# A two-layer mixer and expert network: mixers admitted at 0.9 of the pace, sums of squares closed one piece later, first expert weights and rows loaded earlier

## The chip, the cores and the metric

The kernel runs on one core of a Trainium2 chip. A core has five engines, each with its own queue of instructions that it works off in order: PE (matrix multiply; PEld is its weight load), DVE (VectorE), ACT (ScalarE), POOL (GpSimd) and SP (only transfers here). Transfers (DMA) are issued by SP, ACT and POOL. SBUF is the on-chip memory, PSUM the banks that PE writes, DRAM the chip's large memory. The metric is device time in microseconds (us).

## The reference

`x` has 4 sequences of 1024 tokens with 1024 channels, `f` (fside) the same shape. Two layers follow each other:

```
mix(L) = sigmoid(x or x1) * (nf + nb - ekv + euk*v) / (df + db - ek + euk) * (0.8 + 0.2 tf)
x1  = x + ((mix0 @ weight.T) * scale + bias)
h   = rmsnorm(mix1) * norm_w              # needs the sum of squares over all channels of a token
out = x1 + mix1 + sum over 4 of 32 experts + shared(h)
```

with k = v = f. `nf, df` are forward scans over the tokens (a = a*decay + ek), `nb, db` backward ones. The router takes the four best of 32 experts per token by `h @ router_w.T`; an expert is `(silu(h w1a) * (h w1b)) w2` with inner size 512, the shared one the same with 1024. All is float32.

## The kernel before, in words

**Tokens and channels.** Channels lie on the partitions, 8 tiles (NC) of 128. Tokens go in 8 chunks `q` of 512 (CH), two for each sequence `b`. PE works in *pieces*, most of them 16 matmul instructions of 128x128 by 128x512 into one PSUM bank: `first_ffn(q)` (8 pieces, L431, weights `w0t`, the mixer's output `c0` as moving side), `shared_up(q)` (16, L644) and `shared_down(q)` (8, L672).

**Mixers.** `mixing()` (from L234) is a generator over 64 units (sequence, channel tile, layer). A unit is two forward scans (L280), two backward scans (L292) and some passes on DVE, exponentials and logarithms on ACT, one accumulating transfer `fg<-euk` on POOL (L325), and a store to `c0_d` or `c1_d` in DRAM (L340). A unit of layer 0 also loads `xg` (L334, issued on ACT's queue) and takes its sigmoid on ACT (L223) at the start of the next step. Each `yield` gives the DVE time that the step is held to take (W_SCANS and so on).

**The written order.** Nothing is scheduled at run time. `run()` (L377) walks through the list of pieces from `order()` and writes instructions to the queues in that order. It keeps two running totals, `work["vector"]` and `work["tensor"]`: before each piece it lets mixer steps in while the first is below the second, then writes the piece, then what is due `after` so many pieces, then one step of each stream in `beside`. A piece's loads (`early`) are written two pieces ahead. `mix_until` writes mixer steps at once where a piece needs a unit that is not yet written.

**Gate and sum of squares.** `gate(q, ot, ...)` follows each piece of `first_ffn` (for chunks 0 and 1 it runs later, in `late_gate`): a sigmoid on ACT, a product on DVE into `c1` and its square on ACT (L465, L466), then two accumulating transfers on POOL: `c1` into the residual in DRAM (L469) and, but for chunk 0, the square into the tile `acc` (L473). All eight squares of a chunk go into the same `acc`. `total` then multiplies by ones on PE (L480), which gives the sum over partitions, and starts `norm_route(q)` in `beside`. For chunk 0, `total` is called for each of the eight tiles.

**norm_route(q)**, one step per piece: square root on ACT into `rs`, reciprocal on DVE (L523), the eight tiles scaled on DVE (L526, in two steps of four), the router matmul on PE (L533) and its copy on ACT (L535), then top four (L559, L560), ranks (`chose`, L596, L597), and in four steps `turn_rows`: PE transposes (L544) into the PSUM tiles `tr` (two buffers, also used by L533 and by `turned` of `shared_down`, L677), ACT copies (L546), stores to the row table `h_d`. At the end tokens and shares are scattered to expert slots.

**plan() and the experts.** After the last chunk's routing `plan()` works out which expert and which tokens each block of 128 rows has, in two kinds: pairs of blocks (kind 0) and single ones (kind 1). Then `first_weights` allocates the weight tiles and loads the weights of the first two units, 6 MB each, in six steps. After the pieces come an `If` (L1211) for surplus blocks, which are none in this data, and `run_units`: per unit a gather of the token rows `hs<-h_d` on POOL (L936), transposes (L951), 7 half-size products for gate and up (L1097), the same for down, and an indirect accumulate to DRAM.

**What the change touches by name:** pool sizes `pc0` (buffers of `c0`; 12) and `p1` (holds `rs`), `PACE`, `mix_until`, `run`, `gate`/`total`, `norm_route`, `plan`, `first_weights`, `order`, `Unit.gather`, `run_units`.

Of the kernel before, what the change touches and what calls it, by code (L numbers as in the profile page):

```python
# [8 lines left out]
FP = mybir.dt.float32  # L9
# [13 lines left out]
P = 128  # L23
CH = 512
# [7 lines left out]
def kernel(  # L32
# [157 lines left out]
    def right(name, bufs):  # L190
        return a.enter_context(tc.tile_pool(name=name, bufs=bufs, side="right"))
# [3 lines left out]
    p1 = right("p1", 1)  # L195
    p2 = right("p2", 2)
    pxg = right("pxg", 2)
    pc0 = right("pc0", 2 * NC - 4)
    pc1 = right("pc1", NC)
    px = right("px", 6)  # L200
    pw0 = right("pw0", 3)
# [8 lines left out]
    W_SCANS, W_MIN, W_PASS, W_HALF = 4.7, 0.7, 1.25, 0.75  # L210
    W_PIECE, W_SMALL = 6.9, 1.0
    LATENCY = 12.0
    table = [None]

    def exp_ln(to, of, func, **kw):
# [127 lines left out]


    work = {"vector": 0.0, "tensor": 0.0}
    mixer = mixing()

    def mix():
        step = next(mixer, None)
        if step is None:  # L350
            return False
        work["vector"] += step
        return True

    def mix_until(*wanted):
        while not made.issuperset(wanted):
            assert mix()
            work["tensor"] = max(work["tensor"], work["vector"])

    due = []  # L360
    count, told = [0], [0]
# [1 line left out]
    def after(pieces, f, vector=0.0, tensor=0.0):  # L363

        told[0] += 1
        due.append((count[0] + 1 + pieces, told[0], f, vector, tensor))
# [10 lines left out]
    def run(pieces, ahead=2):  # L377
        for i, piece in enumerate(pieces):
            for p in pieces[i : i + ahead + 1]:
                if p.early:  # L380
                    p.early()
                    p.early = None
            while work["vector"] < work["tensor"] and mix():
                pass
            piece.do()
            work["tensor"] += piece.tensor
            count[0] += 1
            now = sorted(d for d in due if d[0] <= count[0])
# [59 lines left out]
    def gate(q, ot, x, lag=1):  # L448

        b = q // NCH  # L450
        c1 = c1s[q, ot]
        held = {}

        def sigmoid():
            held["y"] = psq.tile([P, CH], FP, name="y")
            other(held["y"], x, AF.Sigmoid, bias=v["b0"][:, ot : ot + 1])


        each = q == 0
        if ot == 0 and not each:  # L460
            accs[q] = pacc.tile([P, CH], FP, name="acc")
        square = accs[q] if ot == 0 and not each else None

        def gated():
            nc.vector.scalar_tensor_tensor(c1, c1, nosc[:, b : b + 1], held["y"], ALU.mult, ALU.mult)  # L465
            nc.scalar.activation(held["y"] if square is None else square, c1, AF.Square)  # L466

        def add():
            nc.gpsimd.dma_start(out=resT_d[ot, :, bass.ts(q, CH)], in_=c1, accum_op=ALU.add)  # L469
            if each:  # L470
                total(held["y"])
            elif square is None:
                nc.gpsimd.dma_start(out=accs[q], in_=held["y"], accum_op=ALU.add)  # L473

        def total(of):
            if of is None:
                of = accs.pop(q)
            if ot == 0 or not each:
                sums[q] = ps_ss.tile([P, CH], FP, name="ss")
            nc.tensor.matmul(  # L480
                sums[q], lhsT=ones, rhs=of, start=(ot == 0 or not each), stop=(ot == NC - 1)
            )
            if ot == NC - 1:
                beside.append(norm_route(q))

        after(lag, sigmoid)
        after(lag + 1, gated, W_HALF)
        after(lag + (3 if each else 2), add, 0.0, W_SMALL if each else 0.0)
        if ot == NC - 1 and not each:
            after(lag + 3, lambda: total(None), 0.0, W_SMALL)  # L490

    def late_gate(q):

# [22 lines left out]
    def norm_route(q):  # L516

        NJ = CH // P
        hs = [c1s[q, ct] for ct in range(NC)]
        rs = p1.tile([P, CH], FP, name="rs")  # L520
        other(rs, sums.pop(q), AF.Sqrt, bias=eps_c, scale=1.0 / C)
        yield 0.0, 0.0
        nc.vector.reciprocal(rs, rs)  # L523
# [1 line left out]
        for ct in range(NC):  # L525
            nc.vector.scalar_tensor_tensor(hs[ct], hs[ct], v["nw"][:, ct : ct + 1], rs, ALU.mult, ALU.mult)  # L526
            if q == NT // CH - 1:
                nc.sync.dma_start(out=hT_d[ct], in_=hs[ct])
            if ct % 4 == 3:
                yield 4 * W_HALF, 0.0  # L530
        lgT_ps = ps_tr.tile([E, CH], FP, name="tr")
        for ct in range(NC):
            nc.tensor.matmul(lgT_ps, lhsT=rw_sb[:, ct, :], rhs=hs[ct], start=(ct == 0), stop=(ct == NC - 1))  # L533
# [163 lines left out]
    def plan():  # L697
# [5 lines left out]
        experts = lists.tile([1, 2, P], I32, name="experts")  # L703
        many = lists.tile([1, 3], I32, name="many")
        have.update(tokens=tokens, shares=shares, experts=experts, many=many)
        with tc.tile_pool(name="plan", bufs=1, side="right") as pl, tc.tile_pool(
            name="ps_pl", bufs=1, space=PSUM
        ) as ps_pl:
# [22 lines left out]
            for kind, n in enumerate((npair, nsing)):  # L731
# [47 lines left out]
                be_ps = ps_pl.tile([P, P], FP, name="pl_ps")  # L779
                nc.tensor.matmul(be_ps[0:1, :], lhsT=be, rhs=ident, start=True, stop=True)  # L780
                nc.vector.tensor_copy(experts[:, kind, :], be_ps[0:1, :])
                yield 0.3, 0.3
                for i, got in enumerate(gots):
                    tk_ps = ps_pl.tile([P, 2, P], FP, name="tk_ps")
# [3 lines left out]
                        )  # L788
                        nc.vector.tensor_copy(to[:, 2 * kind + i, :], tk_ps[:, o, :])
                    yield 0.6, 0.5  # L790
        beside.append(first_weights())


    NK, ND = NC // 2, NI // 2
# [64 lines left out]
        op(t[4], b21, t[2])  # L859
        yield  # L860

    def first_weights():
        pwt = kept.enter_context(tc.tile_pool(name="pwt", bufs=1, side="right"))
        have["w1"] = [
            [pwt.tile([P, NK, 2 * I], FP, name=f"w1_{at}{k}") for k in range(2)] for at in range(2)
        ]
        have["w2"] = [pwt.tile([P, NI, C], FP, name=f"w2_{at}") for at in range(2)]
        have["t_up"] = {i: pwt.tile([P, NK, I], FP, name=f"t_up{i}") for i in (2, 3, 4)}
        have["t_down"] = {i: pwt.tile([P, ND, 512], FP, name=f"t_down{i}") for i in (2, 3, 4)}
        for at in range(2):  # L870
            for _ in load(whole[at], at):
                yield 0.0, 0.0

    def order():

        pieces = first_ffn(0, False) + first_ffn(1, False) + late_gate(0)

        pieces.insert(-1, Piece(lambda: None, tensor=LATENCY / 3))
        pieces += [Piece(lambda: None, tensor=0.5) for _ in range(7)]
        up, gates = shared_up(0), late_gate(1)  # L880
        for i, piece in enumerate(up):
            pieces.append(piece)
            if i % 2 == 1:
                pieces.append(gates.pop(0))
        pieces += gates
        pieces += shared_down(0) + shared_up(1) + shared_down(1)
        pieces += first_ffn(2, True) + first_ffn(3, True) + shared_up(2) + shared_down(2) + shared_up(3)
        for b in range(2, B):
            q = NCH * b
            pieces += first_ffn(q, True) + first_ffn(q + 1, True) + shared_down(q - 1)  # L890
            pieces += shared_up(q) + shared_down(q)
            if b + 1 < B:
                pieces += shared_up(q + 1)
        return pieces
# [15 lines left out]
    with ExitStack() as m:  # L910
# [12 lines left out]
        class Unit:  # L923
# [6 lines left out]
                self.down_sums = sums_down(at) if self.kind == 0 else iter(())  # L930

            def gather(self):
                self.hs = []
                for i in self.lists:
                    hs = phs.tile([P, C], FP, name="hs")
                    nc.gpsimd.indirect_dma_start(  # L936
                        out=hs,
                        out_offset=None,
                        in_=h_d,
                        in_offset=bass.IndirectOffsetOnAxis(ap=tokens[:, i, self.n : self.n + 1], axis=0),  # L940
                    )
                    self.hs.append(hs)

            def turn(self):

# [191 lines left out]
        def rest_of(s):  # L1137
            for _ in s:
                pass

        def run_units(us, loaded, ahead=()):


            if not loaded:
                for u in us[:2]:
                    rest_of(u.load)
                rest_of(us[0].up_sums)
            us[0].gather()
            rest_of(us[0].turn())
            us[0].begin_left()  # L1150
            rest_of(us[0].left)
# [59 lines left out]
        with tc.If(count(2, MAXU[0] + MAXU[1]) > 0):  # L1211
            for kind in range(2):
                extra(kind, WHOLE[kind], count(kind, MAXU[kind]))
            with tc.manual_schedule(engines=ENG):
                for at in range(2):
                    rest_of(load(whole[at], at))
                rest_of(sums_up(0))

# [34 lines left out]
        with tc.manual_schedule(engines=ENG):  # L1253
            for u in main[:2]:
                u.load = iter(())
            main[0].up_sums = iter(())
            run_units(main, True, (ahead_1, ahead_2))

            o = have["w2"][before_last]
# [111 lines left out]
```

## Time and profile before

Median 5170.3 us of 3 runs (5169.01 to 5174.28). The profiled execution took 5172.99 us; its span, from first to last instruction, is 5171.2 us, so 1.8 us lie around it.

| stretch, us | what runs | PE busy of it | DVE busy | mean granted PE clock |
|---|---|---|---|---|
| 0 to 197 | mixers of sequence 0, no matmul | 0.0 | 183.9 | 1.00 |
| 197 to 357 | first layer of chunks 0 and 1, gates of chunk 0 | 130.0 of 160 | 140.6 | 0.88 |
| 357 to 1440 | pieces, with mixers beside them | 1015.4 of 1083 | 930.3 | 0.97 |
| 1440 to 2067 | pieces, mixers done | 620.8 of 627 | 104.9 | 1.00 |
| 2067 to 2085 | change to the experts | 0.3 of 18 | 8.6 | 0.59 |
| 2085 to 5121 | experts | 3029.1 of 3036 | 1750.8 | 1.00 |
| 5121 to 5171 | last chunk's shared part | 44.7 of 50 | 10.1 | 0.98 |

A line of a timeline reads: start, duration, engine, source line, operation, what it writes and reads, how many; in square brackets how long the engine had been idle before it and what ended that. In lists of waits, the three numbers are the sum in us, how often, and the longest.

### The profile page before, as it was taken

The page shows a single profiled execution, that of the slowest core. Times are in us where ns is not written, and L with a number is a line of the kernel's source. Part 1 is how long each engine was busy: PE and PEld are TensorE (multiplying, and loading weights), DVE is VectorE, ACT ScalarE, POOL GpSimd, SP SyncE. Part 2 cuts the span into 40 slices and gives each one's busy share as a digit, 9 for nine tenths or more (in the row PEclk, how much of TensorE's full clock was granted, in tenths as well). Part 3 has the DMA queues.
Part 4 walks back from the last instruction along what each step waited for, and adds up shares of the span by engine and source line. Part 5 has one row for each costly group of instructions (what it writes and reads, how often), then busy time and mean ns, then how long its engine had stood idle before and what let it go on. Part 6 is the DMA issues. An engine that isn't in the chain of part 4 may idle for free.

```text
span 5171.2 us, 36505 instructions
## 1 busy us (share of the span) xinstructions
PE 4840.2 (94%) x12906; PEld 2240.0 (43%) x12906; DVE 3129.2 (61%) x3280; ACT 1432.3 (28%) x1831; POOL 811.7 (16%) x765
## 2 busy tenths in 40 slices
PE   0478999999999999899999999999999999999999
PEld 0123443444444444444444444444444444444444
DVE  9978997899710221566655656565656556565621
ACT  5557666667510120111111111111111111111110
POOL 0113201411310120111111111111111111111100
PEclk9989999999999999999999999999999999999999
DMA  4678678679733854677777676767677777767684
GB/s 137 190 200 199 184 223 256 170 192 285 206 113 106 244 151 154 211 219 236 217 235 230 217 241 210 246 202 247 210 237 216 234 235 215 241 216 238 214 234 123
DMA packets 524210, 1077.76 MB, mean 208 GB/s; under 512 B 30641, under 2 KB 260146, under 8 KB 523410
## 3 DMA queue, kind: packets, MB, share of 16 engines
q1 hardware_dynamic: 386338, 744.70, 42.4%
q0 software_dynamic: 74656, 223.12, 20.6%
q10 hardware_dynamic: 63024, 107.50, 5.9%
q8 instruction: 105, 1.72, 0.1%
q14 instruction: 87, 0.71, 0.0%
HBM read 844.13 MB, written 203.56 MB: 203 GB/s over the span
## 4 chain that ended last, share of the span: by engine, by line
PE 86%; DVE 4%; DMA 4%; ACT 3%; issue 3%; ACTq 0%; POOL 0%; SPq 0%; POOLq 0%; DVEq 0%
PE gA L1097 14%; PE mm L644 13%; PE gB L1097 9%; PE gC L1097 9%; PE dA L1097 7%; PE mm L431 6%; PE mm L672 5%; PE dB L1097 5%; PE dC L1097 5%; PE tr L951 2%; PE gA L985 2%; PE gB L985 2%; PE tr L1034 1%; PE tr L533 1%; DMA xg<-in_xT 1%
## 5 line engine op out<-in xcount | busy, mean ns | idle before, releaser
L644 PE MATMUL mm<-c,wpc 128*128 128x512 f32 x1792 | 785.1, 597 | 8.4 <-issue 5.0
L431 PE MATMUL mm<-c,w0t 128*128 128x512 f32 x1024 | 454.9, 606 | 212.8 <-DMA w0t<-in_w 207.7
L644 PEld LDWEIGHTS mm<-c,wpc 128*128 128x128 f32 x1792 | 340.1, 192 | 429.7 <-issue 421.2
L1097 PE MATMUL gA<-w,hsT 128*128 128x512 f32 x1088 | 490.1, 593 | 0.0
L1097 PE MATMUL gB<-t_up,s_up 128*128 128x512 f32 x1088 | 489.1, 592 | 0.0
L1097 PE MATMUL gC<-w,s_up 128*128 128x512 f32 x1088 | 489.1, 592 | 0.0
L1081 POOL DMA_INDIRECT sum_d<-y,tokens x148 | 302.8, 2046 | 920.6 <-DMA sum_d<-y,tokens 542.8
L672 PE MATMUL mm<-sact,wpc 128*128 128x512 f32 x896 | 394.5, 595 | 9.6 <-DVE sact L653 9.6
L936 POOL DMA_INDIRECT hs<-h_d,tokens x148 | 148.3, 1002 | 1621.4 <-PE tr L951 1548.1
L431 PEld LDWEIGHTS mm<-c,w0t 128*128 128x128 f32 x1024 | 199.0, 195 | 466.2 <-issue 448.9
L1097 PEld LDWEIGHTS gC<-w,s_up 128*128 128x128 f32 x1088 | 206.7, 190 | 260.2 <-issue 260.2
L1097 PEld LDWEIGHTS gB<-t_up,s_up 128*128 128x128 f32 x1088 | 206.7, 190 | 260.2 <-issue 244.4
L831 DVE TENSOR_TENSOR t_up<-w,w 128x2048 f32<-128x2048 f32 x136 | 310.6, 2284 | 0.0
L1097 PEld LDWEIGHTS gA<-w,hsT 128*128 128x128 f32 x1088 | 201.8, 191 | 228.2 <-issue 228.2
L292 DVE TENSOR_TENSOR_SCAN fg<-decay,tail,fg 128x1024 f32<-128x1024 f32 x128 | 292.8, 2328 | 0.0
L672 PEld LDWEIGHTS mm<-sact,wpc 128*128 128x128 f32 x896 | 167.7, 191 | 207.5 <-issue 196.9
L1097 PE MATMUL dB<-t_down,s_down 128*128 128x512 f32 x544 | 256.9, 594 | 0.1
L1097 PE MATMUL dA<-w,actT 128*128 128x512 f32 x544 | 255.8, 592 | 0.0
L1097 PE MATMUL dC<-w,s_down 128*128 128x512 f32 x544 | 255.8, 592 | 0.0
L952 ACT COPY hsT<-tr 128x512 f32<-128x512 f32 x296 | 172.6, 588 | 299.6 <-PE tr L951 299.6
L1097 PE MATMUL gA<-t_up,hsT 128*128 128x512 f32 x544 | 244.5, 592 | 0.0
L1022 ACT ACTIVATE act<-c 128x512 f32<-128x512 f32 x68 | 42.9, 630 | 708.9 <-DVE c L1018 708.9
(242 smaller groups left out, 6199.0 us busy)
## 6 DMA issues: line engine op xcount, KB each, us to landing
w<-in_w SPq DMA_DIRECT2D x240, 2048.0 KB
fg<-euk POOLq DMA_DIRECT2D x64, 512.0 KB
c_d<-r ACTq DMA_DIRECT2D x64, 512.0 KB
c<-c_d SPq DMA_DIRECT2D x128, 256.0 KB
w0t<-in_w SPq DMA_DIRECT2D x64, 512.0 KB
wpc<-in_sg SPq DMA_DIRECT2D x56, 512.0 KB
wpc<-in_su SPq DMA_DIRECT2D x56, 512.0 KB
wpc<-in_sd SPq DMA_DIRECT2D x56, 512.0 KB
```

The source lines that it names most:

```text
L292: nc.vector.tensor_tensor_scan(fg[:, m, ::-1], decay[L][:, ct, b : b + 1].to_broadcast([P, T]), fg[:, m, ::-1], tail[:, m : m + 1], ALU.mu ...
L431: nc.tensor.matmul(mm, lhsT=tiles[ot][:, it, :], rhs=c0s[it], start=(it == 0), stop=(it == NC - 1))
L533: nc.tensor.matmul(lgT_ps, lhsT=rw_sb[:, ct, :], rhs=hs[ct], start=(ct == 0), stop=(ct == NC - 1))
L644: nc.tensor.matmul(mm, lhsT=wts[f, n][:, kt, :], rhs=c1s[q, kt], start=(kt == 0), stop=(kt == NC - 1))
L672: nc.tensor.matmul(mm, lhsT=wts[ct][:, f, :], rhs=acts[q, f], start=(f == 0), stop=(f == NSI - 1))
L831: nc.vector.tensor_tensor(to, x, y, ALU.subtract)
L936: nc.gpsimd.indirect_dma_start(out=hs, out_offset=None, in_=h_d, in_offset=bass.IndirectOffsetOnAxis(ap=tokens[:, i, self.n : self.n + 1], ...
L951: nc.tensor.transpose(tr[:, r, :], hs[:, bass.ts(4 * q + r, P)], ident)
L952: nc.scalar.copy(self.hsT[:, 4 * q : 4 * q + 4, b, :], tr)
L985: nc.tensor.matmul(ps, lhsT=self.hsT[:, k, 0, :], rhs=w[k // NK][:, k % NK, bass.ts(n, I)], start=(k == 0), stop=(k == NC - 1),)
L1081: nc.gpsimd.indirect_dma_start(out=sum_d, out_offset=bass.IndirectOffsetOnAxis(ap=tokens[:, i, self.n : self.n + 1], axis=0), in_=y, in_of ...
L1097: nc.tensor.matmul(ps, lhsT=x[:, k, :], rhs=w[:, k, :], start=(k == 0 and not more), stop=(k == half - 1), skip_group_check=more,)
```

## The change

Five edits go together. (1) From the end of the first stage on, mixer steps are let in only while `work["vector"]` is below 0.9 times `work["tensor"]`; a new empty piece `slower` sets this. (2) `total` of a chunk is written four pieces after the gate's sigmoid rather than three, and `norm_route` scales the eight tiles in one step rather than two, so the router matmul stays where it was among the pieces; for chunk 0 it stands one piece earlier. (3) `rs` takes the place of the chunk's `acc` tile (chunk 0 gets one too) instead of a tile of `p1`, and `pc0` has 13 buffers rather than 12. (4) The weight tiles are allocated at the start of `plan()`, and `first_weights` starts when the experts of kind 0 are known; it takes four steps. (5) The token rows of the first unit are gathered within `plan()`, once the tokens of kind 0 are known, into two tiles (`t_down`) that are not needed until later; after surplus blocks, if there are any, they are gathered again.

```
-    pc0 = right("pc0", 2 * NC - 4)
+    pc0 = right("pc0", 2 * NC - 3)
+    PACE = 0.9
+    pace = [1.0]
     def mix_until(*wanted):
-            work["tensor"] = max(work["tensor"], work["vector"])
+            work["tensor"] = max(work["tensor"], work["vector"] / pace[0])
     def run(pieces, ahead=2):
-            while work["vector"] < work["tensor"] and mix():
+            while work["vector"] < pace[0] * work["tensor"] and mix():
     def gate(q, ot, x, lag=1):
-        if ot == 0 and not each:
+        if ot == 0:
             accs[q] = pacc.tile([P, CH], FP, name="acc")
         def total(of):
-                of = accs.pop(q)
+                of = accs[q]
-            after(lag + 3, lambda: total(None), 0.0, W_SMALL)
+            after(lag + 4, lambda: total(None), 0.0, W_SMALL)
     def norm_route(q):
-        rs = p1.tile([P, CH], FP, name="rs")
+        rs = accs.pop(q)
...
-            if ct % 4 == 3:
-                yield 4 * W_HALF, 0.0
+        yield NC * W_HALF, 0.0
     def plan():
+        weights_places()
...
                 nc.vector.tensor_copy(experts[:, kind, :], be_ps[0:1, :])
+                if kind == 0:
+                    beside.append(first_weights())
                 yield 0.3, 0.3
...
                     yield 0.6, 0.5
-        beside.append(first_weights())
+                if kind == 0:
+                    have["first"] = [
+                        gather(have["t_down"][2 + i].rearrange("p k f -> p (k f)"), i, whole[0][1]) for i in range(2)
+                    ]
+    def gather(to, i, n):
+        nc.gpsimd.indirect_dma_start(
+            out=to,
+            out_offset=None,
+            in_=h_d,
+            in_offset=bass.IndirectOffsetOnAxis(ap=have["tokens"][:, i, n : n + 1], axis=0),
+        )
+        return to
     def first_weights():
         for at in range(2):
-            for _ in load(whole[at], at):
-                yield 0.0, 0.0
+            for step, _ in enumerate(load(whole[at], at)):
+                if step == 1:
+                    yield 0.0, 0.0
+            yield 0.0, 0.0
     def order():
         pieces += [Piece(lambda: None, tensor=0.5) for _ in range(7)]
+        def slower():
+            pace[0] = PACE
+            work["tensor"] = max(work["tensor"], work["vector"] / PACE)
+        pieces.append(Piece(slower, tensor=0.0))
     def run_units(us, loaded, ahead=()):
             if not loaded:
...
-            us[0].gather()
+                us[0].gather()
...
+            main[0].hs = have["first"]
             run_units(main, True, (ahead_1, ahead_2))
```

More of the change, by code (lines that the diff above doesn't have):

```diff
@@ L860, in sums_down, with weights_places @@
         yield
-    def first_weights():
+    def gather(to, i, n):
[6 more added lines that the diff above has]
+        return to
+    def weights_places():
         pwt = kept.enter_context(tc.tile_pool(name="pwt", bufs=1, side="right"))
@@ L869, in first_weights @@
         have["t_down"] = {i: pwt.tile([P, ND, 512], FP, name=f"t_down{i}") for i in (2, 3, 4)}
+    def first_weights():
         for at in range(2):
-            for _ in load(whole[at], at):
-                yield 0.0, 0.0
+            for step, _ in enumerate(load(whole[at], at)):
+                if step == 1:
+                    yield 0.0, 0.0
+            yield 0.0, 0.0
     def order():
@@ L932, in gather @@
             def gather(self):
[L933 to L942, printed above, removed]
+                self.hs = [
+                    gather(phs.tile([P, C], FP, name="hs"), i, self.n) for i in self.lists
+                ]
             def turn(self):
@@ L1217 @@
                 rest_of(sums_up(0))
+                for i, hs in enumerate(have["first"]):
+                    gather(hs, i, whole[0][1])
         last = NT // CH - 1
```

## The prediction

> **What bounds the kernel now.** I read the busy time by stretch first. PE is busy 3029.1 of 3036 us in the experts' stretch, which the change leaves as it is, and 620.8 of 627 us from 1440 to 2067. What can move is PE's idle time elsewhere: 67.6 us from 357 to 1440, where the mixers run beside the pieces, and 18 us at the change to the experts. The windows:
>
> ```profile
> 357.00:1440.00 1083.00, 1015.42 (x2564) 454.37 (x2565) 930.29 (x850) 680.25 (x690) 235.51 (x282) 0.97 0.76 210
> 1440.00:2067.00 627.00, 620.79 (x1590) 281.11 (x1590) 104.90 (x247) 72.57 (x112) 81.42 (x129) 1.00 0.51 152
> ```
>
> After the length come PE, PEld, DVE, ACT, POOL, clock, DMA share, GB/s: DVE is 86% busy (930 of 1083), so not the bound on average. The list of PE's waits from 335 to 2060 says who is late:
>
> ```profile
> PE ss L480 <- DMA acc<-y: 15.7, 4, 8.1
> PE tr L544 <- ACT rT L678: 13.7, 7, 8.3
> PE mm L672 <- DVE sact L653: 9.6, 1, 9.6
> PE tr L544 <- ACT hr L546: 8.5, 3, 7.9
> PE mm L431 <- DMA w0t<-in_w: 7.8, 2, 4.1
> PE mm L431 <- DVE fg L323: 5.0, 1, 5.0
> ```
>
> PE's timeline gives the places, and what a wait costs after it ends: 16 matmuls take 7.03 us in a steady run, but 9.11 after the wait at 597.
>
> ```profile
> 257.99 56.70 PE L431 MATMUL mm<-c,w0t 128*128 128x512 f32 x128 [2.68 <-DMA w0t<-in_w]
> 510.32 16.51 PE L672 MATMUL mm<-sact,wpc 128*128 128x512 f32 x34 [9.60 <-DVE sact L653]
> 597.34 1.11 PE L544 MATMUL tr<-ident,c 128*128 128x128 f32 x4 [8.27 <-ACT rT L678]
> 598.24 9.11 PE L644 MATMUL mm<-c,wpc 128*128 128x512 f32 x16
> 860.62 2.08 PE L480 MATMUL ss<-acc,ones 128*128 128x512 f32 x2 [8.05 <-DMA acc<-y]
> 921.73 2.11 PE L544 MATMUL tr<-ident,c 128*128 128x128 f32 x8 [7.94 <-ACT hr L546]
> 1752.82 36.21 PE L431 MATMUL mm<-c,w0t 128*128 128x512 f32 x80 [3.69 <-DMA w0t<-in_w]
> ```
>
> ACT's timeline shows why it is late at 921: it waits for the load `xg` that it issued just before, with the row copies behind it in its queue. The same pair stands before the waits at 510 and 597.
>
> ```profile
> 906.25 0.34 ACTq L334 DMA_DIRECT2D xg<-in_xT  x1
> 914.88 1.06 ACT L223 ACTIVATE xg<-xg 128x1024 f32<-128x1024 f32 x1 [4.40 <-DMA xg<-in_xT]
> ```
>
> Last, the chain of waits at 2067 to 2085: POOL is released at 2074.38, issues the gather, and its landing releases PE.
>
> ```profile
> 2074.46 0.04 POOLq L936
> 2074.50 0.10 issue
> 2074.60 1.90 POOL hs L936
> 2076.50 0.30 issue
> 2076.80 8.35 DMA hs<-h_d,tokens
> 2085.15 0.18 issue
> 2085.32 3.78 PE tr L951 x16
> ```
>
> **The change part by part.**
>
> A, later `total`. It gets one piece, 6.87 us, more. The four waits on `acc` are 8.05, 5.64, 1.47 and 0.54; three go, 1.2 of the first stays: 14.5 saved. The matmuls behind the two long ones ran 1.4 and 2.1 us over steady pace (22.14 and 22.86 for 48 against 20.77), so 18. Behind `total` come the root (0.7), the reciprocal (3.3) and eight scalings (5.4 in one run at 361) on ACT and DVE; the router matmul now stands three pieces, 20.6 us, after `total` instead of four. At 862.7 to 881.1 root to last scaling took 18.4 us with two gates in between, of which the single step drops one. It fits by some 3 us. Ends: 0, if the wait moves there, and 19.
>
> B, row copies (L544). Waits 13.7 + 8.5 = 22.2, with slow work behind them (2.1 at 598, 1.1 + 1.5 at 921, 1.7 at 1424) 28.6. Only the mixers' places change. In the changed order of ACT's queue the pair `xg` load and sigmoid no longer stands before the first row copies of chunks 1 and 2, nor among those of chunk 5; at chunk 3 it now stands between the second and the third set, which gives up what exceeds a piece (8.3 - 6.87 = 1.4), and at chunk 4 it still stands ahead. I take the two long waits, 8.27 + 2.1 + 7.94 + 2.6, less 1.4: 20. Ends 0 and 28.6.
>
> C, 9.60 at 510 plus 1.9 slow (16.51 for 34 against 14.6): the last Silu of chunk 0 now stands ahead of the `xg` pair. I take 10; ends 0 and 11.5.
>
> D, chunk 0's routing a piece earlier: `chose` gets a further piece, its wait (2.9, seen at 398) goes; the small transposes come straight behind the router matmul and wait for its copy (0.6 plus the hand-over, 0.8). 2; ends -1 and 3.
>
> E, 13 buffers of `c0`. At the start of chunks 1, 3, 5, 7 PE waited 2.68, 4.10, 5.05 (put down to DVE), 3.69: the last four `c0` loads on SP wait for buffers that the last piece before frees one by one (0.86 us apart), and `w0t` stands behind them in SP's queue. With three late ones `w0t` is issued 0.86 us sooner behind 256 KB less (0.8 us at the 303 GB/s around 260). At most 4 x 1.7 = 6.8; I take 5. Ends 0 and 6.8. I leave the slow restart of some 1.9 us each in place, since 257.99 shows it after 2.68 us of idling (56.70 against 55.10).
> The Trainium skill, TensorE: Matmul & The Clock Gate (What's actually happening), lets the clock drop only after about 3.4 us without work; by that the four shortened waits would mostly fall below the bound and E would bring up to 7.6 more, which the row at 257.99 speaks against.
>
> F, the gather. Its issue (1.90 + 0.95 us) moves to POOL's idle time before 2010, where only one further gather is behind it (28.96 us idle there). PE's last transposes end at 2067.28; it reaches the far side of the `If` at 2074.38, as POOL's release shows, and then waits 10.9 us more. What is late next: DVE ends the four weight sums at 2075.68, and if its way through the `If` also takes 7.1 us, the row sums start at 2082.8 and the second product, which reads them, at 2084.2 instead of 2093.2. I take 9; ends 5 and 11.
> The Trainium skill, Advanced Engine Details and Errata (Control Flow Timing), puts a compare-and-branch at about 108 ns; if the branch were all, PE would have been through at 2067.4 and F would be worth nearly the whole 18 us. The 7.1 us in the trace include the load of the counts and whatever else lies there, so I keep to the row.
>
> G, weights earlier. Their 12 MB now stand on SP between the `wpc` loads from about 1991 instead of from 2038; SP also waits for the cast of `experts` (1990.70 before), with `wpc` behind it. A 4.2 MB set at the mean 359 GB/s of 2038 to 2068 takes 11.7 us, and a `wpc` behind it 1.5 more, against two pieces (13.7) of lead. -1; ends -5 and 0. The first weight sums waited for nothing before, so nothing is won.
>
> H, mixers where there were none. The last mixer step stands 18 pieces later. In 616 to 816 and 1040 to 1197, with mixers but no routing, PE's only wait was one of E; one new hit of the kind in B costs 8.3 + 2. I take -8; ends -20 and 0.
> Mixers do not come too late: the layer-0 units of sequence 1 are all written four pieces (28 us) before the piece that reads them, before it was nine; `mix_until` forces nothing after the first stage in either order.
>
> Sum: 18 + 20 + 10 + 2 + 5 + 9 - 1 - 8 = 55. The span goes from 5171.2 to 5116; with 1.8 around it 5118, and the median lay 2.7 under the profiled run: 5115.
>
> **The rivals.**
>
> R1, the ACT waits only move. Speaks for it: of 24 `xg` loads of sequences 1 to 3, 15 had no other ACT work before their sigmoid, and 14 still have none. Against: three of the 15 reached PE, and the new order clears those three. B and C gone: 5145.
>
> R2, the wait of A comes back at the router matmul, as the margin is 3 us: 5129 to 5133.
>
> R3, slower: the pairs of R1 hit PE more often than before. A hit costs 8.27 + 2.1 = 10.4 us. Without B and C 25 us of gain are left; to be 10 us slower needs 35, and with H's hit already in, eight hits among the 14 pairs decide. Three were seen, so 5185 is far off.
>
> R4, the pace changes nothing at all because ACT and DVE are late for other reasons, and E and F stay small: 5160 to 5172.
>
> **How the numbers follow.** Forecast 0.66 (its own range 5097 to 5132, by the ends of B, F and H); R1 0.15; R2 0.07; R4 0.05; R3 0.07. The range reaches to R1: 5094 to 5147. It leaves out R3, R4 and the outer part of R1. A change under 0.2% (10 us) can't be told from none here; faster 0.88, same 0.05, slower 0.07.
>
> **What would show it.** No wait of L480 on `acc` over 2 us; no wait of L544 over 3 us at chunks 1 and 2; no wait at the first piece of `shared_down(0)`; waits at the chunk starts 1 to 2 us shorter; first transpose of the experts about 7 us after the last of the pieces; PE idle from 357 to 1440 down from 67.6 to under 35, with mixers until about 1490. It is wrong if L533 starts to wait for DVE, if L544 or L644 wait for ACT elsewhere, or if L672 waits for `wpc` behind the weights.

## The result, and the profile after

The changed kernel takes 5107.5 us, the median of 4 runs (5104.2 to 5110.8), against 5169.7 us (5167.0 to 5174.3) for the kernel before beside it: ratio 0.9879, 95% interval 0.9862 to 0.9896. The forecast was 5115.0, its range 5094 to 5147. The profiled execution took 5109.81 us, its span is 5107.8 us; the span before was 5171.2, so 63.4 us went, where 55 were forecast. One execution of the kernel before, in the last set of runs below, took 18,516 us, and it is left out of all times and ratios.

All of it went before the experts. Their first transposes start at 2022.42 us instead of 2085.32, 62.9 us earlier; the experts after that take as long as before. The windows of the changed kernel, cut at that point (columns: length, PE, PEld, DVE, ACT, POOL, clock, DMA share, GB/s):

```profile
0.00:357.00 357.00, 127.51 (x272) 52.92 (x272) 326.79 (x246) 208.09 (x203) 44.50 (x59) 0.95 0.65 185
357.00:1440.00 1083.00, 1062.04 (x2721) 478.44 (x2722) 897.90 (x838) 668.46 (x682) 251.60 (x310) 0.99 0.77 211
1440.00:2022.40 582.40, 561.13 (x1435) 253.34 (x1434) 144.15 (x262) 95.52 (x128) 71.94 (x104) 0.99 0.58 175
```

Between 357 and 1440, PE's idle time fell from 67.6 to 21.0 us (1083.0 - 1062.0). DVE does less there (897.9 against 930.3) and more behind 1440: the mixers have been spread further. PE's idle time up to the first transposes of the experts fell by 47.1 us in all (318.9 before, 271.7 after: lengths less PE's busy time in the three rows, and the same for before with 2085.3 as the last edge). Its *busy* time up to there fell as well, by 15.8 us (1766.5 to 1750.7), though it does the same work. 47.1 + 15.8 = 62.9.

The busy time is shown by the groups of PE's lines up to 2085 us, all of one form (count, busy us, mean ns; then idle time before them). Before:

```profile
L431 PE MATMUL mm<-c,w0t 128*128 128x512 f32 x1024 | 454.9, 606 | 212.8 <-DMA w0t<-in_w 207.7 <-DVE fg L323 5.0
L644 PE MATMUL mm<-c,wpc 128*128 128x512 f32 x1792 | 785.1, 597 | 8.4 <-issue 5.0 <-ACT sact L223 3.1 <-DMA wpc<-in_su 0.3
```

and after:

```profile
L433 PE MATMUL mm<-c,w0t 128*128 128x512 f32 x1024 | 447.9, 599 | 213.9 <-DMA w0t<-in_w 212.4 <-DVE c L467 1.5
L645 PE MATMUL mm<-c,wpc 128*128 128x512 f32 x1792 | 777.7, 593 | 0.9 <-DMA wpc<-in_su 0.9
```

1024 and 1792 matmuls each time, but 7.0 and 7.4 us less. The mean granted clock from 357 to 1440 rose from 0.97 to 0.99: fewer of them run at a low clock behind a wait.

The list of PE's waits after (sum, times, longest), of which the kernel before had 15.7 us on `acc`, 22.2 before the row copies and 9.6 on `sact`. The first line is the gates of chunk 0, 20.0 us before, which the change leaves as they were:

```profile
PE ss L482 <- ACT y L468: 19.8, 3, 16.2
PE mm L433 <- DMA w0t<-in_w: 13.4, 2, 8.1
PE tr L971 <- DVEq L1231: 11.6, 1, 11.6
PE tk_ps L790 <- DVE tokens L793: 7.5, 3, 6.2
PE tr L534 <- DVE c L528: 5.0, 1, 5.0
PE tr L545 <- ACT rT L679: 3.9, 5, 2.9
PE mm L433 <- DVE c L467: 1.5, 1, 1.5
...
PE tr L545 <- ACT hr L547: 0.6, 2, 0.4
```

No wait on `acc` (L482 after) is left, none of L673 on `sact`. What is left stands at the starts of chunks, in the last pieces and at the change to the experts; PE's timeline gives the places:

```profile
255.85 55.17 PE L433 MATMUL mm<-c,w0t 128*128 128x512 f32 x128 [1.91 <-DMA w0t<-in_w]
569.72 1.11 PE L545 MATMUL tr<-ident,c 128*128 128x128 f32 x4 [2.92 <-ACT rT L679]
789.87 43.67 PE L433 MATMUL mm<-c,w0t 128*128 128x512 f32 x96 [5.32 <-DMA w0t<-in_w]
1213.50 43.49 PE L433 MATMUL mm<-c,w0t 128*128 128x512 f32 x96 [8.11 <-DMA w0t<-in_w]
1969.96 0.49 PE L790 MATMUL tk_ps<-ident,got 128*128 128x128 f32 x1 [6.18 <-DVE tokens L793]
2022.42 3.78 PE L971 MATMUL tr<-ident,t_down 128*128 128x128 f32 x16 [11.59 <-DVEq L1231]
```

On ACT, the pair of `xg` load and sigmoid at chunk 3 now stands between the second and the third pair of row copies, as the prediction read from the changed order. The sigmoid waits less for its load, 1.30 us against 4.40, and PE had the whole of it to spare (no wait of L545 there):

```profile
887.01 0.59 ACT L547 COPY hr<-tr 128x512 f32<-128x512 f32 x1 [0.45 <-ACT hr L547]
...
891.64 0.34 ACTq L335 DMA_DIRECT2D xg<-in_xT  x1
...
895.56 1.06 ACT L224 ACTIVATE xg<-xg 128x1024 f32<-128x1024 f32 x1 [1.30 <-DMA xg<-in_xT]
...
898.75 0.56 ACT L547 COPY hr<-tr 128x512 f32<-128x512 f32 x1
```

### The profile page after: what moved, and what is told of

Its sections match the earlier page's. It is cut to its first block, busy times and chain, and to the rows that moved or that the text cites. A ratio compares the mean times of both kernels' runs of the same rounds, so it can differ in the third digit from the quotient of the medians.

```text
span 5107.8 us, 36503 instructions
## 1 busy us (share of the span) xinstructions
PE 4823.9 (94%) x12906; PEld 2235.0 (44%) x12906; DVE 3130.7 (61%) x3280; ACT 1445.5 (28%) x1840; POOL 818.4 (16%) x765
## 4 chain that ended last, share of the span: by engine, by line
PE 60%; ACT 0%; issue 0%; DVE 0%; ACTq 0%
PE gA L1117 14%; PE gC L1117 9%; PE gB L1117 9%; PE dA L1117 7%; PE dB L1117 5%; PE dC L1117 5%; PE tr L971 2%; PE gA L1005 2%; PE gB L1005 2%; PE tr L1054 1%; PE dA L1067 1%; PE dB L1067 1%; PE gB L1305 0%; PE gC L1305 0%; PE gA L1305 0%; PE dA L1305 0%
## 5 line engine op out<-in xcount | busy, mean ns | idle before, releaser
L673 PE MATMUL mm<-sact,wpc 128*128 128x512 f32 x896 | 395.2, 596 | 0.0
L838 DVE TENSOR_TENSOR t_up<-w,w 128x2048 f32<-128x2048 f32 x136 | 310.7, 2285 | 0.0
L673 PEld LDWEIGHTS mm<-sact,wpc 128*128 128x128 f32 x896 | 168.1, 191 | 198.2 <-issue 196.7
```

The costliest lines, as they stand in the source:

```text
L673: nc.tensor.matmul(mm, lhsT=wts[ct][:, f, :], rhs=acts[q, f], start=(f == 0), stop=(f == NSI - 1))
L838: nc.vector.tensor_tensor(to, x, y, ALU.subtract)
```

## The experiments

All times are medians of 4 runs (5 for the runs at eight tenths and with both repairs), with the kernel before at 5169.8, 5171.2 and 5170.9 us beside them. The changed kernel, run once more with the last of them, took 5105.2 us, and its two profiled executions differ by 5.2 us (5109.8 and 5104.6). Differences of under about 5 us are thus at the edge of what these runs settle; where the median says little, PE's waits are given.

### Is it the order?

Theory: the pace alone removes most of the waits. Rival: the other edits are needed for it. Three runs: the change without the pace, the pace without the change, and a slower pace still.

**Change without the pace.**

```
-    PACE = 0.9
+    PACE = 1.0
```

> The changed kernel with PACE 1.0, so the mixers go in at full pace and all else is changed. Theory (the slower pace clears ACT and DVE waits): PE idle from 357 to 1440 goes from 21 us back to 45 or more, with waits of L545 and L673 again, and the time is 25 to 40 us over the changed kernel: 5133 to 5148. Rival (the later total and the new order of chunk 0 did it, pace has no part): within 8 us of 5107.

Measured: 5146.1 us (5145.1 to 5151.3), ratio 0.9953 (0.9937 to 0.9970), 38.6 us over the changed kernel. From the list of PE's waits, those on ACT and on `sact` are back:

```profile
PE tr L545 <- ACT rT L679: 15.3, 7, 8.7
PE mm L673 <- DVE sact L654: 9.7, 1, 9.7
```

PE is idle for 53.9 us between 357 and 1440 (1083 - 1029.07), against 21.0. The wait on `sact` stands where it stood before, at the first piece of `shared_down(0)` (501 us). The long one before a row copy (8.7) now stands at 1338, in chunk 5, not at 597 in chunk 1: at full pace, which copy is hit depends on the order. On `acc` 4.5 us are left of 15.7, so the later `total` cures most of that wait without the pace.

**The pace alone**, in the kernel before:

```
+    PACE = 0.9
-            work["tensor"] = max(work["tensor"], work["vector"])
+            work["tensor"] = max(work["tensor"], work["vector"] / pace[0])
-            while work["vector"] < work["tensor"] and mix():
+            while work["vector"] < pace[0] * work["tensor"] and mix():
+        pieces.append(Piece(slower, tensor=0.0))
```

> The kernel before with the written order at nine tenths as the only edit (total at lag + 3, 12 buffers of c0, weights and gathers as before). Theory: the order alone ends the waits of L544 on ACT, of L672 on DVE and most of those of L480 on acc, since these come from where the mixers stand; the full change without the order still lost 39 us of its 62. So 5125 to 5135, and what is left to the full change is mainly the If (some 7 us) and single waits on acc. Rival: the order needs the later total to work, the waits on acc stay near 15 us in all: 5140 to 5150.

Measured: 5122.1 us (5119.7 to 5127.1), ratio 0.9907 (0.9891 to 0.9924): 49 of the 62 us. The time lies 3 us below the theory's band, far from the rival's. The waits left:

```profile
PE tr L959 <- DMA hs<-h_d,tokens: 17.6, 1, 17.6
PE mm L433 <- DMA w0t<-in_w: 8.8, 2, 5.6
PE ss L482 <- DMA acc<-y: 6.1, 3, 3.1
...
PE tr L546 <- ACT hr L548: 2.3, 1, 2.3
PE tr L546 <- ACT rT L680: 2.0, 5, 1.0
```

The wait on `sact` is gone, the waits before the row copies are down from 22.2 to 4.3, and those on `acc` from 15.7 to 6.1 without `total` being moved. So the crowding of mixer steps also has a part in what sends `acc` late. The pace alone is worth 49 us and the change without it 24, 73 together, and both 62: in part they cure the same waits.

**Eight tenths** in the changed kernel (`PACE = 0.8`).

> The changed kernel with the written order at eight tenths of VectorE's time instead of nine. Theory: what counts is that the mixers are thinned out, so that ACT's and DVE's steps for the pieces are no longer behind them; nine tenths has cleared nearly all of that (the waits of L545 on ACT add up to 4.5 us, those of L673 on DVE to none), so eight tenths finds nothing more to gain, 5103 to 5112. Rival: the gain is a matter of where single pairs of load and sigmoid happen to fall in ACT's queue; another pace throws them anew, and one to four hits of 10 us come back: 5118 to 5148.

Measured: 5141.2 us (5137.6 to 5145.1), ratio 0.9943 (0.9929 to 0.9957), 36 us over the changed kernel beside it (5105.2). The theory as I put it, that a slower pace finds nothing to gain and loses nothing, fell. The number is in the rival's range, but its mechanism doesn't carry it: the waits before row copies add up to 9.5 us against 4.5. The large ones are elsewhere:

```profile
735.56 1.09 PE L678 MATMUL tr<-ident,rT 128*128 128x128 f32 x4 [8.40 <-DVE rT L687]
742.05 8.78 PE L433 MATMUL mm<-c,w0t 128*128 128x512 f32 x16 [5.41 <-DMA w0t<-in_w]
1180.68 57.67 PE L433 MATMUL mm<-c,w0t 128*128 128x512 f32 x128 [11.16 <-ACT ek L220]
```

742 and 1180 are the first pieces of chunks 2 and 4, each the first chunk of a sequence, which read that sequence's layer-0 units. The changed kernel goes over both without a wait (at 728.57 and 1150.29). At eight tenths the units are not written in time, and `mix_until`, which writes whatever is missing at once, can only put it in front of these pieces. DVE's timeline shows the pile: a backward scan and the passes of L311 to L325 with the next scans stand without a break of more than 2.52 us before the one step that PE waits for,

```profile
730.30 2.29 DVE L281 TENSOR_TENSOR_SCAN fg<-decay,ek 128x1024 f32<-128x1024 f32 x1
732.50 2.27 DVE L281 TENSOR_TENSOR_SCAN fg<-decay,ekv 128x1024 f32<-128x1024 f32 x1
734.68 0.73 DVE L687 SCALAR_TENSOR_TENSOR rT<-mm,v_b,rT 128x512 f32<-128x512 f32 x1
```

Going through `run()` with the kernel's own step times, `mix_until` writes seven steps at once ahead of the loads of each of these two pieces at eight tenths; at nine tenths and in the kernel before it writes none there. The pace has two sides, then: at ten tenths the mixers crowd the pieces' small steps, at eight their own deadline is missed, and nine lies between. How much of nine tenths' gain over ten is luck in where single pairs of load and sigmoid fall is not shown, as no pace between was run: the waits before row copies are 19.0 us at ten tenths, 4.5 at nine and 9.5 at eight.

### What is the later `total` worth?

```
-            after(lag + 4, lambda: total(None), 0.0, W_SMALL)
+            after(lag + 3, lambda: total(None), 0.0, W_SMALL)
-        yield NC * W_HALF, 0.0
+            if ct % 4 == 3:
+                yield 4 * W_HALF, 0.0
```

> The changed kernel with total again at three pieces and the scalings in two steps. Theory (one more piece hides the accumulating transfers): waits of the sum-of-squares matmul on acc of 10 to 16 us come back, with slow restarts 14 to 19 us: 5121 to 5126. Rival (with the slower pace ACT and POOL are early enough, the wait would be gone anyway): 0 to 5 us, 5107 to 5112.

Measured: 5116.3 us (5113.1 to 5119.8), ratio 0.9899 (0.9882 to 0.9915), 8.7 us over the changed kernel's first median and 11.1 over its second. It lies between the two forecasts: waits on `acc` come back, but 6.5 us of them, not 15.7.

```profile
PE ss L482 <- DMA acc<-y: 6.5, 2, 4.9
```

The later `total` and the pace cure the same wait; each takes what the other leaves (4.5 us without the pace, 6.5 here, none with both).

### The gather and the weights

The gather (edit 5) and the start of the weights (edit 4) were put back one at a time, then both. The four steps of `first_weights`, instead of six, and the early allocation of its tiles stay in all three.

Gather late: the two gathers after the tokens and their use in the first unit are taken out, and the first unit gathers after the `If` again.

```
-                if kind == 0:
-                    have["first"] = [
-                        gather(have["t_down"][2 + i].rearrange("p k f -> p (k f)"), i, whole[0][1]) for i in range(2)
-                    ]
-            main[0].hs = have["first"]
```

> The changed kernel with the first unit's rows gathered after the If again, weights still early. Theory: the first transposes wait about 18 us after the last piece instead of 11.6, time 6 to 8 us over the changed kernel: 5114. Rival (the way through the If on DVE sets the start, the gather is hidden): 0 to 2 us.

Measured: 5106.2 us (5102.8 to 5109.7), ratio 0.9875 (0.9858 to 0.9891): nothing lost.

Weights late:

```
-                if kind == 0:
-                    beside.append(first_weights())
...
+        beside.append(first_weights())
```

> The changed kernel with first_weights started after plan() as before, rows still early. Theory (early weights only crowd the queue of SP): the 6.2 us wait of the token transposes for DVE goes, 4 to 7 us under the changed kernel: 5101 to 5104. Rival (the weights then come late for the first sums or products): 3 us or more over it.

Measured: 5110.5 us (5107.5 to 5112.4), ratio 0.9884 (0.9868 to 0.9901): 3 to 5 us slower, if anything. The theory fell: the wait on `tokens` went, as it said, but a longer one came (10.8 us, in the table below).

Both late (the two diffs together):

> The changed kernel with both the gather of the first rows and the first weights put back to where they were before; the order, the later total and the buffers stay. Theory, from the runs that put back one of them and lost nothing to 3 us: each makes up for the other, since rows and weights gathered and loaded in the same microseconds share the DMA; with both late the first transposes wait some 18 us on hs again instead of 11.6, and the time is 6 to 9 us longer, 5112 to 5117. The prediction's F less G, taken apart from what DVE costs: 8 us, 5115. Rival: neither is worth anything, 5104 to 5110.

Measured: 5112.0 us (5106.0 to 5113.4), ratio 0.9882 (0.9866 to 0.9898), against 5105.2 (5104.6 to 5112.7) for the changed kernel on the same chip. 6.8 us slower, at the lower edge of what the theory gave, and the ranges overlap. Its reason was wrong: the first transposes wait 9.9 us for `hs`, not 18. The waits at the end of the pieces, in us:

| kernel | small transposes, on `tokens` | `turned` of the last pieces, on DVE's `rT` | first transposes of the experts | sum |
|---|---|---|---|---|
| before | 1.7 | 0.3 | 18.1 | 20.1 |
| changed | 7.5 | - | 11.6 | 19.1 |
| gather late | 3.9 | - | 11.2 | 15.1 |
| weights late | 1.7 | 10.8 | 11.1 | 23.6 |
| both late | 1.7 | 10.3 | 9.9 | 21.9 |
| pace alone | 1.7 | - | 17.6 | 19.3 |

From PE's timeline, the two long waits with both late:

```profile
2011.95 1.09 PE L678 MATMUL tr<-ident,rT 128*128 128x128 f32 x4 [10.33 <-DVE rT L687]
2022.90 1.94 PE L966 MATMUL tr<-ident,hs 128*128 128x128 f32 x8 [9.86 <-DMA hs<-h_d,tokens]
```

Two things follow. In the changed kernel and these three runs the wait of the first transposes is 10 to 12 us; the early gather does not shorten it. With the gather late, the first rows land 5 to 6 us after POOL issues them (2016.90 to 2022.77 in both late), against some 10 with the pace alone (2025.14 to 2035.34), where the weights go out in six steps until 2014. And wherever the 12 MB of weights are loaded in four steps, some `rT` load of the last pieces stands behind them on SP and comes late. In the kernel before and with the pace alone, in six steps, PE waits 0.3 us for `rT` or not at all. So the four steps, two weight loads at once, are the likely reason; a run with six steps and the rest of the change was not made. From SP's timeline of the changed kernel:

```profile
1950.43 0.96 SPq L819 DMA_DIRECT2D w<-in_w  x2
1951.49 1.80 SPq L666 DMA_DIRECT2D wpc<-in_sd  x1
1953.35 9.31 SPq L670 DMA_DIRECT2D rT<-resT_d  x1
```

and of its DVE, where the copy of `tokens` that PE waits for comes straight behind the late `rT`:

```profile
1968.96 0.75 DVE L687 SCALAR_TENSOR_TENSOR rT<-mm,v_b,rT 128x512 f32<-128x512 f32 x1 [12.34 <-DMA rT<-resT_d]
1969.63 0.28 DVE L793 CAST tokens<-tk_ps 128x128 int32<-128x128 f32 x1
```

Early weights put the delay where PE loses 6.2 us of it, late ones where it loses 10.3 to 10.8. By the sums of the table, edits 4 and 5 together bring PE 1 us or less here.

### The thirteenth buffer

```
-    pc0 = right("pc0", 2 * NC - 3)
+    pc0 = right("pc0", 2 * NC - 4)
```

> The changed kernel with 12 buffers of c0 again. Theory, from the trace after, where the waits at the chunk starts did not get shorter (1.91, 5.32 and 8.11 against 2.68, 4.10 and 5.05): the thirteenth buffer is worth nothing, 5105 to 5110 and the waits at the chunk starts 2 to 8 us as they are. The prediction's term E: 5 us slower, 5112 to 5113, each of the waits 1 to 2 us longer.

Measured: 5111.7 us (5106.8 to 5119.4), ratio 0.9887 (0.9870 to 0.9903). The median is where the term E put it, the intervals overlap with those of the changed kernel. The waits at the starts of chunks 1, 3, 5 and 7 are 3.69, 4.67, 8.64 and 2.89 us, 19.9 in all, against 1.91, 5.32, 8.11 and 1.48, 16.8. Two of them have a slow restart behind them that the changed kernel doesn't have (55.17 for 128 matmuls, 41.44 for 96):

```profile
259.32 57.93 PE L433 MATMUL mm<-c,w0t 128*128 128x512 f32 x128 [3.69 <-DMA w0t<-in_w]
1691.28 43.14 PE L433 MATMUL mm<-c,w0t 128*128 128x512 f32 x96 [2.89 <-DMA w0t<-in_w]
```

3.1 us of waits, and 3.1 of restarts over the four places (2.8 and 1.7 here, 0.7 and 0.6 less at the other two), make 6.2. In the other profiled executions with 13 buffers and this order (the changed kernel's second, gather late, weights late, both late, and the early sums below) the four waits add up to 15.6 to 17.4 us, so 19.9 lies outside. My theory that the buffer is worth nothing, drawn from the comparison of before and after, is thus not borne out: by the medians the buffer is worth 4 to 6 us in the new order, by the waits some 3 without restarts, and the overlap of the times leaves the size open. Something else in the change has cost about as much of these waits. Chunk 5 points to it. Its wait is 4.3 to 5.1 us in the three kernels with `total` at `lag + 3` (before, the pace alone, the earlier `total`), and 7.4 to 9.7 in all with `lag + 4` in which `w0t` stands behind the `c0` loads, except at eight tenths, where PE had waited 11.16 us just before (2.79). With `total` alone put back the four waits are 13.5 us. How the later `total` lengthens the wait was not followed up.

### The waits that are left

**Weight sums before the `If`.** The four sums of the first unit (L838) are written among the pieces, behind their loads:

```
         yield 0.0, 0.0
+        for _ in sums_up(0):
+            yield 2.3, 0.0
...
-        for _ in sums_up(0):
-            pass
```

> The changed kernel with the four weight sums of the first unit written among the pieces, behind their loads, instead of at the start of the experts. Theory: in the changed kernel PE's first transposes of the experts wait 11.6 us for DVE, which ends those sums at 2019.1 and only then goes through the If; with the sums done before, DVE comes free with the last pieces, the wait falls to 5 to 6 us (another engine's way through the If), and the time by 5 to 7 us: 5100 to 5103. Rival: the sums among the pieces make DVE late for a piece instead, or the next thing after the If is as late: 5106 to 5112.

Measured: 5106.0 us (5103.4 to 5109.2), ratio 0.9876 (0.9859 to 0.9892). The wait did what the theory said:

```profile
2015.48 4.11 PE L971 MATMUL tr<-ident,t_down 128*128 128x128 f32 x16 [5.89 <-ACTq L1231]
```

5.89 us instead of 11.59. The time did not follow as clearly: the median is 1.5 us under the changed kernel's first and 0.8 over its second. By itself this run leaves the gain open.

**`w0t` ahead of the `c0` loads.**

```
             if ot == 0:
                 mix_until(*((b, ct, 0) for ct in range(NC)))
...
+                tiles[ot] = pw0.tile([P, NC, P], FP, name="w0t")
+                nc.sync.dma_start(out=tiles[ot], in_=w0[ot])
                 for ct in range(NC):
...
-            tiles[ot] = pw0.tile([P, NC, P], FP, name="w0t")
-            nc.sync.dma_start(out=tiles[ot], in_=w0[ot])
+            if ot > 0:
+                tiles[ot] = pw0.tile([P, NC, P], FP, name="w0t")
+                nc.sync.dma_start(out=tiles[ot], in_=w0[ot])
```

> The changed kernel with the first w0t of a chunk's first layer issued on SP ahead of the chunk's c0 loads instead of behind them. Theory: the waits at the first piece of chunks 1, 3 and 5 (1.91, 5.32 and 8.11 us) are the place of w0t in SP's queue, behind loads that wait for buffers: they go, and the time falls by 10 to 17 us, to 5091 to 5098. Rival: the DMA engines are full in these stretches (share 1.0), the last c0 loads are as late and take the wait over: within 4 us of the changed kernel.

Measured: 5103.0 us (5095.1 to 5104.6), ratio 0.9865 (0.9849 to 0.9882): 2.2 to 4.5 us below the changed kernel. SP issues that `w0t` at 771.84 instead of 780.65 at chunk 3, and the first piece there no longer waits. The second does: it waits 5.69 us for its own `w0t`, which still stands behind the `c0` loads.

```profile
796.16 36.59 PE L436 MATMUL mm<-c,w0t 128*128 128x512 f32 x80 [5.69 <-DMA w0t<-in_w]
1211.19 1.12 PE L436 MATMUL mm<-c,w0t 128*128 128x512 f32 x2 [0.46 <-DMA c<-c_d]
1215.88 36.27 PE L436 MATMUL mm<-c,w0t 128*128 128x512 f32 x80 [3.57 <-DMA w0t<-in_w]
```

The waits at chunks 1 and 7 are gone, chunk 5 keeps 4.03 of 8.11. It lies between theory and rival: of the 16.8 us at the four places 9.7 are left, and the DMA share is 1.04 from 760 to 800.

**Both repairs together.**

> The changed kernel with the first w0t ahead of the c0 loads and the weight sums of the first unit among the pieces, both at once. Theory: the two are far apart and each shortens a wait of PE, 4 to 8 us at the chunk starts and 5.7 us at the If, so they add: 5094 to 5100. Rival: the wait at the If is not shorter for the time, as the medians of the run with the sums alone differ by only 1.5 us: 5102 to 5105.

Measured beside the changed kernel on one chip:

> The changed kernel once more, as the yardstick for the three runs beside it on one chip: 5104 to 5111, as it had.

The changed kernel 5105.2 us (5104.6 to 5112.7), ratio 0.9877 (0.9861 to 0.9893); with both repairs 5095.0 us (5088.6 to 5100.3), ratio 0.9853 (0.9839 to 0.9867). The runs do not overlap: 10 us, at the theory's better end. Together they are worth more than the medians of the two alone let one expect, and this version is faster than both kernels. PE's idle time from 1440 to 2100 us is 13.9 us in it, against 21.8 in the changed kernel.

## Why the prediction came out

The time was 7.5 us below the forecast, well inside its range and inside the forecast's own. (That one's slow end, 5132, does not follow from its terms: the ends of B, F and H give 5151. Nothing hangs on it here.) The likeliest case was what happened: the mixers' new places removed the waits (R4 is refuted by the pace alone, R1 by the waits themselves, R2 and R3 by waits that did not appear). But the sum of 55 came near 63.4 by terms that missed on both sides.

**What bounds the kernel** was right. Everything came out of the time before the experts, 47.1 us of it out of PE's idle time and 15.8 out of its busy time, and the forecast "67.6 to under 35" was met with 21.0.

**A, later `total` (18).** All 15.7 us of waits on `acc` went. The rival R2, the return of the wait at the router matmul, did not come: L534 waits 5.04 us at chunk 0, as L644 did before (5.00), and not after that. That L533 waits for DVE was named as a sign of being wrong; it showed at chunk 0 only, with the pace alone too, in place of a wait of the same length, and cost nothing. The size was right, the cause only half: the pace alone takes 9.6 us of the 15.7, the rest of the change alone 11.2.

**B, row copies (20).** 22.2 us of waits fell to 4.5, and the two long ones named are gone. Right. That the pair of load and sigmoid in ACT's queue was the cause is borne out by where the waits went with the pace and came back without it; a run with the pair alone moved was not made.

**C (10).** The wait of 9.60 went, and with it a 3.09 before L644 at 467 that I had not counted. 12.7 in all.

**D (2).** 2.90 and 0.28 became 0.67. Right in size; but the wait for `chose` is gone as well with the pace alone, whose empty piece `slower` already lets the router matmul run ahead of the piece it stood behind, so the earlier `total` of chunk 0 is not shown to be its reason.

**E, 13 buffers (5).** The waits at the chunk starts did not get shorter against the kernel before: 15.5 there, 16.8 after. Yet without the buffer they are 19.9, with slower restarts. The buffer does what E said it does: in the new order the eight `c0` loads of a chunk take 0.7 to 2.9 us less to issue with it (0.2 to 1.9 in the changed kernel's second execution), and `w0t` goes out behind them. SP's timeline at chunk 3 with 13 buffers,

```profile
771.54 9.06 SPq L422 DMA_DIRECT2D c<-c_d  x8
780.65 0.43 SPq L424 DMA_DIRECT2D w0t<-in_w  x1
```

and with 12:

```profile
771.28 11.91 SPq L422 DMA_DIRECT2D c<-c_d  x8
```

The failed step is what it was subtracted from. I took the four waits as they stood before and shortened each by up to 1.7, while the same change moved what else loads there: at chunk 3, with 12 buffers in the old order, the eight loads took only 7.31 us. E also counted itself apart from A, and the later `total` took some 3 back at chunk 5 (4.26 us with it put back, 7.4 to 8.1 in the changed kernel).

**F and G, gather and weights (9 less 1).** This is where the reasoning failed. F itself nearly came: the second product of the first unit starts 18.9 us after the last transposes of the pieces (2010.84 to 2029.73), 25.9 before (2067.28 to 2093.20), so 7.0 for 9; and what is late next is DVE's way through the `If`, as named. But the first transposes start 11.6 us after the last ones, not about 7, and the runs show that the 7.0 do not hang on the gather: put back alone it costs nothing, and the second product still starts 18.9 us after (2011.01 to 2029.88). And G was mis-priced: I looked for a late `wpc` behind the weights and found two pieces of lead. The late one is the `rT` load. DVE stands idle for it for 12.34 us, and the delay reaches PE through the copy of `tokens`, whose waits rose from 1.7 to 7.5 us: 5.8 for 1. F less G gave 1.2 us for 8.

The Trainium skill, Advanced Engine Details and Errata (Control Flow Timing), gives a compare-and-branch about 108 ns. With DVE's sums out of the way PE still waits 5.89 us from its last transposes of the pieces to the first behind the `If`, released by another engine's queue at the same line. In this program the way through the `If` is thus much longer than a branch, as the row of the prediction said.

**H, new hits (8).** None came. The largest new wait before row copies is 2.92 us, at 569.72.

**Slow restarts.** I had 8.6 us of them in the terms (3.5 in A, 4.7 in B, 0.4 in C). PE's busy time fell by 15.8, of which 2.5 lie before 357 us, where the first row alone takes 54.2 to 56.3 us from kernel to kernel. This is one of the terms I under-sized most.

So: the waits of A to D gave 48.6 us where their terms, without the 8.6 of restarts, held 41.4, 7.2 more; restarts up to 7.2 more than counted; H 8 more: 22.4 in all. Against that E gave -1.3 for 5 and F less G 1.2 for 8, 13.1 less. That the sum came within 8.4 us is in part luck: more than half of the excess was cancelled by E, F and G.

## What to carry to other kernels

In an order written ahead of time, background work does not have to fill its engine: let in at nine tenths of the rate, it cleared waits that single edits had been aimed at, and the first thing to look at is its deadline, which eight tenths missed. When a load is moved earlier, go through every later load of its queue and follow the latest one to who reads it, since here it was not the one with the tightest lead that hurt. And a buffer or a wait that looks worthless in a comparison of before and after should be undone alone before it is called so: other edits had taken back what it gave.

## What the runs showed that was not expected

**A wait often costs more than its length, here mostly from about 2.7 us on.** Behind the waits of 1.35 to 2.66 us at the starts of chunks 1 and 7, the matmuls ran at the steady pace (55.17 us for 128, 41.44 for 96), with two exceptions (1.91, then 56.87; 2.57, then 56.63). Behind 2.68 (56.70), 2.86 (58.16), 2.89 (43.14) and 3.69 (57.93) they took 1.5 to 3.0 us longer. The bound is not sharp: a wait of 2.79 cost nothing (20.84 for 48 against 20.77), nor did one of 3.17 with the pace alone (55.17). In the kernel before, the mean granted clock from 258 to 262, behind the wait of 2.68, was 0.61. The Trainium skill, TensorE: Matmul & The Clock Gate (What's actually happening), puts the drop behind an idle window of about 3.4 us; here it came behind shorter ones, so that a wait trimmed from 3 to 2 us can save more than the microsecond.

**The weights slow the queue, not only the DMA.** The issue of one `rT` load on SP took 9.31 us behind the weights of the experts, against about 0.5 us when they are through.
